# Graph attention, then masked attention: the first stage of x with VectorE transposes and seven block products for both matrices

## The chip, the cores and the metric

The kernel runs on one core of a Trainium2 chip, as one launch. The core has TensorE (matmuls, into PSUM), VectorE, ScalarE and GpSimd (elementwise work; in profiles DVE, ACT and POOL), and SyncE (SP), from which most DMAs of this kernel are issued. The metric is the device time of one execution in microseconds (us); lower is better. All data are 32-bit floats unless a smaller type is named.

## The reference

Two layers over 4096 nodes with 512 features, and an adjacency matrix of 4096 x 4096 zeros and ones. Cut to what is computed:

```python
# layer 0: graph attention, H = 4 heads of D = 128
support = (x @ weight).reshape(N, H, D).transpose(1, 0, 2)
f1 = einsum('hnd,hdo->hn', support, weight_u)[:, None, :]
f2 = einsum('hnd,hdo->hn', support, weight_v)[:, :, None]
logits = f1 + f2
w = where(logits >= 0, logits, 0.2 * logits)
masked = w * adj[None]; mask = masked != 0
attn = softmax(where(mask, masked, -1e30), axis=-1) * mask
out = einsum('hij,hjd->hid', attn, support) -> (N, H * D)
x1 = layernorm(x + out + bias + x @ proj_w + proj_b)
# layer 1: 8 heads of 64, keys, queries and values of x1, masked by adj with its diagonal
scores = einsum('hqk,hmk->hqm', x1 @ Wq, x1 @ Wk) / 8
att = softmax(scores + 0.01 * eye - 1e16 * (1 - max(adj, eye)))
result = layernorm(x1 + einsum('hqm,hmk,hko->qo', att, x1 @ Wv, Wo))
```

The change concerns the first two products, `x @ weight` (the support) and `x @ proj_w` (the projection), the two dot products of the support with `weight_u` and `weight_v`, and the sum x + bias + projection + proj_b (here the base).

## The kernel before, in words

The order of all instructions is written by hand: `tc.manual_schedule()` keeps, on each engine and on each DMA queue, the order in which the Python code issues them. An engine that waits for a semaphore holds everything behind it. A helper `later.at(n, fn)` puts work off by n steps, and `later.step()` counts the steps and issues what is due.

**First stage (lines 638 to 893).** x is worked in 8 groups of 512 rows (`for g in range(NG)`), each of 4 tiles of 128 rows. `load_x` brings 4 tiles with 4 DMAs, two groups ahead. `turn_x` (726) makes the transposed x of the next group: TensorE transposes 128x128 blocks into PSUM, VectorE and ScalarE copy them out in turn. For the first group the support is four plain products per tile (871). For the seven others it is seven block products instead of eight (Strassen's scheme, `block_product`, 807): x is cut in 2x2 blocks (row half, feature half), as is the weight, each product is 4 matmuls of 256 columns, and sums of blocks are formed before (`combine_x` on VectorE, 784; `combine_w` on GpSimd, 754) and after (ScalarE 823 and 827, GpSimd 825 to 834, VectorE 836). The projection (877) is 16 matmuls of 512 columns a group, and its base is made of the PSUM result and x plus bias, which GpSimd has added before (853), in one VectorE sum (886).

`dots` (795) multiplies a block of the support by the vectors (801, 512 wide) and reduces it (803), twice a block (weight_u, weight_v), all on VectorE.

`factors` (665) follows at the end of each group. ScalarE takes exponentials of the dot sums (669 to 680), VectorE notes their range (682, 683), GpSimd scales the support by them (685 to 689), SP stores it. Three steps later (`rest`, 694) the row factors are transposed by TensorE, copied and stored.

`beside` sets further work at given tiles: GpSimd starts DMAs that turn the adjacency into 16 bits (`narrow`, 585), SP transposes it by DMA (591), ScalarE turns it into 8 bits (597). At tile 30 the first three steps of the next stage are prepared (`front`, 617).

**Second stage (L1016 and its helpers)**: 4 windows of 1024 rows x 4 heads = 16 passes of 32 steps. In each step VectorE makes the weights p (633, 628) from ScalarE's signs (624), and TensorE multiplies them with the scaled support. `add_base` (980) adds the base by an accumulating DMA, `close` normalises. **Third stage**: keys, queries and values, then masked attention; the change does not touch it.

## Time and profile before

| what | before |
|---|---|
| median of 3 runs | 3380.09 us (3379.16 to 3389.31) |
| span of the profiled execution, first to last instruction | 3376.2 us |
| TensorE busy | 3351.0 us, 99% |
| VectorE busy | 2405.8 us, 71% |
| ScalarE busy | 1991.2 us, 59% |
| GpSimd busy | 2244.8 us, 66% |
| mean granted TensorE clock | 0.997 |
| first stage ends on TensorE | 232.2 us from the span's start |
| second stage runs without a gap from | 245.4 us |

The profile gives one execution's span; no time of its own is listed beside it for that execution. The median of the runs shown is 3.9 us above the span. Lines of the profile name an instruction by its line in the kernel, its engine, and the tiles it writes and reads (`out<-in`). In the timeline the columns are start, duration, engine, line, operation and, in brackets, how long the engine had been idle and what released it. A duration reaches from start to end, and the next instruction on the same engine may begin before that end. TensorE's work on 32-bit floats shows two records for each matmul.

### The profile page before, as it was taken

What the parts mean: (1) busy time and instruction counts of PE and PEld (TensorE: products, weight loads), DVE (VectorE), ACT (ScalarE), POOL (GpSimd) and SP (SyncE); (2) the same over time, 40 slices, a digit from 0 to 9 for tenths busy, and PEclk for the clock granted to TensorE, in tenths of its full rate; (3) what the DMA queues carried; (4) which work ended last, traced back from release to release, by engine and by line L of the source; (5) the groups of instructions that cost most, each with busy time, mean ns of one, the idle gap of its engine ahead of it and who ended that gap; (6) DMA issues with size and microseconds to landing.
All of it is one profiled execution on the core that took longest, in us unless ns stands there. A gap on an engine that the chain in (4) does not pass through costs nothing.

```text
span 3376.2 us, 66035 instructions
## 1 busy us (share of the span) xinstructions
PE 3351.0 (99%) x26970; PEld 1921.4 (57%) x26970; DVE 2405.8 (71%) x2485; ACT 1991.2 (59%) x2468; POOL 2244.8 (66%) x1592
## 2 busy tenths in 40 slices
PE   9999999999999999999999999999999999999998
PEld 5669999999999855543333333333333333333332
DVE  6889899998898721157766767666676666667676
ACT  1347877878876421156665656656566656656564
POOL 5650021030030174569999999999999999999996
PEclk9999999999999999999999999999999999999999
DMA  7989979769451263388989898899989889898884
GB/s 192 202 157 159 183 195 213 172 141 210 132 163 64 42 210 111 115 223 193 211 193 223 223 212 194 201 207 233 215 190 211 195 199 254 192 211 192 205 198 111
DMA packets 397129, 620.36 MB, mean 184 GB/s; under 512 B 165520, under 2 KB 242576, under 8 KB 395792
## 3 DMA queue, kind: packets, MB, share of 16 engines
q0 software_dynamic: 97376, 258.50, 42.2%
q1 hardware_dynamic: 298912, 356.49, 35.4%
q8 instruction: 214, 3.51, 0.4%
q10 hardware_dynamic: 528, 1.05, 0.1%
q14 instruction: 99, 0.81, 0.1%
HBM read 315.87 MB, written 117.64 MB: 128 GB/s over the span
## 4 chain that ended last, share of the span: by engine, by line
PE 97%; DVE 1%; DMA 1%; ACT 0%; POOL 0%; issue 0%; SPq 0%; POOLq 0%; DVEq 0%
PE o_ps L1016 27%; PE o_ps L1329 26%; PE s_ps L1067 26%; PE s_ps L1132 5%; PE s_ps L1393 3%; PE o_ps L877 3%; PE s_ps L1125 3%; PE o_ps L818 2%; DMA wq<-in_L_gnn_Wqs_dram 1%; PE s_ps L1348 1%; PE o_ps L871 0%; PE x_ps L997 0%; PE x_ps L735 0%; DVE p L1461 0%; PE x_ps L1125 0%; DVE x_sb L784 0%
## 5 line engine op out<-in xcount | busy, mean ns | idle before, releaser
L1304 POOL TENSOR_TENSOR q_sum<-q_sum,p 128x1024 f32<-128x1024 f32 x538 | 1375.8, 2557 | 62.2 <-DMA p<-p 39.0
L1284 DVE TENSOR_TENSOR p<-s_ps,adjT 128x1024 f32<-128x1024 f32 x896 | 1043.7, 1216 | 466.2 <-ACT s_ps L1281 443.4
L1281 ACT ACTIVATE s_ps<-s_ps 128x1024 f32<-128x1024 f32 x1021 | 967.1, 1006 | 594.5 <-PE s_ps L1067 594.3
L1329 PE MATMUL o_ps<-p,v_sb 64*64 64x512 f32 x8192 | 943.6, 590 | 0.0
L1067 PE MATMUL s_ps<-q_sb,k_sb 64*64 64x512 f32 x8192 | 942.7, 589 | 0.0
L1016 PE MATMUL o_ps<-sup_t,p 128*128 128x129 f32 x8192 | 922.3, 275 | 3.9 <-DVE p L633 3.9
L1016 PEld LDWEIGHTS o_ps<-sup_t,p 128*128 128x128 f32 x8192 | 919.7, 192 | 4.9 <-DVE p L633 3.9
L633 DVE SCALAR_TENSOR_TENSOR p<-fr_t,dj,az 128x1024 f32<-128x1024 f32 x512 | 654.6, 1288 | 80.9 <-PE o_ps L1016 53.5
L1329 PEld LDWEIGHTS o_ps<-p,v_sb 64*64 64x64 f32 x8192 | 310.3, 133 | 570.6 <-issue 560.3
L1067 PEld LDWEIGHTS s_ps<-q_sb,k_sb 64*64 64x64 f32 x8192 | 312.8, 133 | 565.9 <-issue 457.0
L624 ACT ACTIVATE z<-fr_t,f 128x1024 fp8e4<-128x1024 f32 x512 | 558.0, 1144 | 120.1 <-DVE az L628 119.7
L1314 POOL DMA_DIRECT2D p<-p x412 | 438.3, 1303 | 10.0 <-PE o_ps L1329 8.4
L980 POOL DMA_DIRECT2D agg<-base_d x32 | 28.6, 1201 | 526.8 <-ACT agg L967 526.6
L1284 DVE TENSOR_TENSOR p<-s_ps,md 128x1024 f32<-128x1024 f32 x128 | 150.5, 1217 | 67.3 <-ACT s_ps L1281 63.4
L628 DVE TENSOR_TENSOR az<-adjT,z 128x512 int32<-128x512 int32 x256 | 176.0, 688 | 4.1 <-ACT z L624 3.4
L584 POOL COPY seen<-token 128x1 f32<-128x1 f32 x24 | 14.0, 582 | 240.1 <-DVE token L582 240.1
L1139 ACT ACTIVATE sb<-s_ps 128x1024 f32<-128x1024 f32 x35 | 35.8, 1024 | 188.6 <-PE s_ps L1132 125.9
L597 ACT ACTIVATE adjT<-stage 128x1024 fp8e4<-128x1024 bf16 x128 | 130.9, 1050 | 4.5 <-DMA stage<-adj_d 4.5
L1154 POOL TENSOR_TENSOR sb<-sb,sb 128x1024 f32<-128x1024 f32 x36 | 84.4, 2359 | 71.7 <-ACT sb L1139 71.7
L877 PE MATMUL o_ps<-pw_sb,xT 128*128 128x512 f32 x256 | 115.1, 592 | 0.0
L1178 DVE COPY k_sb<-s_ps 128x1024 f32<-128x1024 f32 x12 | 14.7, 1224 | 139.2 <-PE s_ps L1132 89.5
L1393 PE MATMUL s_ps<-wo_sb,on 128*128 128x512 f32 x240 | 110.8, 604 | 0.0
(164 smaller groups left out, 2171.7 us busy)
## 6 DMA issues: line engine op xcount, KB each, us to landing
p<-p POOLq DMA_DIRECT2D x412, 512.0 KB, 9.1
k_sb<-k_d SPq DMA_DIRECT2D x128, 512.0 KB, 8.0
v_sb<-v_d SPq DMA_DIRECT2D x128, 512.0 KB, 5.9
adj_d<-in_adj_dram POOLq DMA_DIRECT2D x32, 1024.0 KB, 12.3
sup_t<-sup_d SPq DMA_DIRECT2D x120, 258.0 KB, 7.3
fr_t<-fr_d SPq DMA_DIRECT2D x16, 1024.0 KB, 7.5
adjT_d<-adjT SPq DMA_DIRECT2D x32, 512.0 KB, 4.5
adjT<-adjT_d SPq DMA_DIRECT2D x32, 512.0 KB, 6.7
```

The source lines that it names most:

```text
L624: nc.scalar.activation(z[:, k, :], fr[:, 0, :], AF.Sign, bias=fs[j // GT][:, 0, (j + k) % GT, h:h + 1], saturate=False)
L628: nc.vector.tensor_tensor(az.bitcast(I32), adjT[w, j // CJ][:, j % CJ:j % CJ + 2, :].bitcast(I32), z.bitcast(I32), op=ALU.bitwise_and)
L633: nc.vector.scalar_tensor_tensor(p, fr[:, 1, :], dj[j // GT][:, j % GT, h:h + 1], az_t[w, h, j // 2][:, j % 2, :], op0=ALU.max, op1=ALU.mult)
L877: nc.tensor.matmul(b_ps, xT[:, c, t * P:(t + 1) * P], pw_sb[c], start=(c == 0), stop=(c == KC - 1))
L1016: nc.tensor.matmul(o[t // BK][:, t % BK, :], p[:, t * P:(t + 1) * P], s, start=(j == 0 and t % BK == 0), stop=(j == NT - 1), skip_group_ch ...
L1067: nc.tensor.matmul(s[c:c + MS, e, :], k[r, a + c:a + c + MS], qt[g, m][r, :], start=True, stop=True)
L1281: nc.scalar.activation(s, s, AF.Exp)
L1284: nc.vector.tensor_tensor(p, s, keep[:, None, :].to_broadcast([P, HP, G]), op=ALU.mult)
L1304: nc.gpsimd.tensor_tensor(q, q, p, op=ALU.add)
L1314: later.at(2, lambda: nc.gpsimd.dma_start(a, b, accum_op=ALU.add))
L1329: nc.tensor.matmul(o[c, n, :], v[r, j % CH, c], p[r, e, :], start=(j == 0), stop=(j == NT - 1))
L1393: nc.tensor.matmul(s, on_t[g][:, m, t * P:(t + 1) * P], wo_sb[:, m, :], start=(m == 0), stop=(m == NP1 - 1))
```

## The change

1. x is loaded in another layout (`y_sb`): in blocks of 32 rows, four DMAs a group, so that four VectorE instructions, each transposing 32x32 blocks over 128x512, give the transposed x. The features lie in another order over the partitions, and the two matrices are loaded in the same order (eight DMAs each in place of four). TensorE transposes nothing in this stage.
2. Support and projection are both made by seven block products in all 8 groups, with a scheme that shares its sums (`product`): one set of four sums of x (two on VectorE, two on GpSimd) serves both matrices, and each matrix has four sums of weights. The order of the 14 products is in `usual`, and for the first group in `begin`.
3. The residual x is part of the projection: the identity is added to `proj_w` in 16 small GpSimd instructions at the start.
4. In `dots`, the multiplication by `weight_u` moves to GpSimd; the one by `weight_v` and both reductions stay on VectorE.
5. `factors` is put off by a step into the next group (after the fourth product), except in the last group. The row factors are transposed on VectorE in 32x32 blocks and stored with four DMAs.
6. bias and proj_b are no longer in the stage. In the first pass of the second stage, GpSimd issues eight accumulating DMAs that add their sum to the stored base, one per group.

```diff
-    base_d = [dram.tile([P, D], F32, name=f"base_d{i}") for i in range(NT)]
+    base_d = [dram.tile([P, GT, D], F32, name=f"base_d{g}") for g in range(NG)]
...
-            def load_x(g):
-                for t in range(GT):
-                    i = g * GT + t
-                    xs[i] = sp.tile([P, D], F32, name="x_sb", bufs=3 * GT)
-                    nc.sync.dma_start(xs[i], x[i * P:(i + 1) * P, :])
-            load_x(0)
-            for c in range(KC):
-                nc.sync.dma_start(w_sb[c], weight[c * P:(c + 1) * P, :])
-            for c in range(KC):
-                nc.sync.dma_start(pw_sb[c], proj_w[c * P:(c + 1) * P, :])
+            ys, xTs = {}, {}
+            def load_x(g, halves=1):
+                ys[g] = sp.tile([P, G // SQ, P], F32, name="y_sb", bufs=3)
+                nb = G // SQ // halves
+                for n in range(halves):
+                    r0 = g * G + n * nb * SQ
+                    for a in range(NQ):
+                        nc.sync.dma_start(
+                            ys[g][a * SQ:(a + 1) * SQ, n * nb:(n + 1) * nb, :],
+                            x[r0:r0 + nb * SQ, a * P:(a + 1) * P].rearrange(
+                                "(b r) f -> r b f", r=SQ))
+                    yield
...
+            halves = load_x(0, 2)
+            next(halves)
+            load_w0(w_sb, weight, 0)
+            next(halves)
+            load_w0(w_sb, weight, 1)
+            for c in range(2):
+                load_w0(pw_sb, proj_w, c)
             nc.sync.dma_start(uv[:, 0, :], on_all_partitions(weight_u, D))
             nc.sync.dma_start(uv[:, 1, :], on_all_partitions(weight_v, D))
-            nc.sync.dma_start(bb[:, 0, :], on_all_partitions(bias, D))
-            nc.sync.dma_start(bb[:, 1, :], on_all_partitions(proj_b, D))
-            load_x(1)
-            sums_of_w = wp.tile([P, 2, W], F32, name="fr_t").rearrange("p k r -> p (k r)")
-            last_fr = sums_of_w[:, 3 * D:4 * D]
+            list(load_x(1))
...
-                    nc.tensor.transpose(p, fr.rearrange("p k h t -> p (k h t)"), ident)
-                    if end:
-                        row = last_fr[0:n, P:2 * P]
-                    else:
-                        row = sp.tile([n, P], F32, name="fr_row")
-                    nc.vector.tensor_copy(row, p)
+                    n = 2 * H0 * GT
+                    row = sp.tile([P, n], F32, name="fr_row")
+                    nc.vector.transpose(row, fr.rearrange("p k h t -> p (k h t)"))
                     r0 = g * G % W
-                    nc.sync.dma_start(
-                        fr_d[g * G // W][:, :, r0:r0 + G].rearrange(
-                            "k h (t r) -> (k h) t r", r=P), row)
-                later.at(9 if end else 3, rest)
+                    dst = fr_d[g * G // W][:, :, r0:r0 + G].rearrange(
+                        "k h (t a r) -> a (k h) t r", a=NQ, r=SQ)
+                    for q in range(NQ):
+                        nc.sync.dma_start(dst[q], row[q * SQ:(q + 1) * SQ, :])
+                if g + 1 < NG:
+                    later.at(1, rest)
+                else:
+                    rest()
...
+            def turn_x(g, c, n=0, halves=1):
+                if c == 0 and n == 0:
                     xTs[g] = sp.tile([P, KC, G], F32, name="xT")
-                if g == 0:
-                    p = op.tile([P, G], F32, name="o_ps").rearrange("p (t r) -> p t r", t=GT)
+                nb = G // SQ // halves
+                nc.vector.transpose(
+                    xTs[g][:, c, n * nb * SQ:(n + 1) * nb * SQ].rearrange(
+                        "p (b r) -> p b r", r=SQ),
+                    ys[g][:, n * nb:(n + 1) * nb, c * SQ:(c + 1) * SQ])
...
-                for t in range(GT):
-                    nc.tensor.transpose(p[:, t, :], xs[g * GT + t][:, c * P:(c + 1) * P], ident)
-                dst = xTs[g][:, c, :]
-                if c % 2:
-                    nc.vector.tensor_copy(dst, p.rearrange("p t r -> p (t r)"))
-                else:
-                    nc.scalar.activation(dst, p.rearrange("p t r -> p (t r)"), AF.Copy)
...
+            def combine_w(engine, kind):
+                w = w_sb if kind == "s" else pw_sb
+                t1, t2, t3, t4 = sums_w[kind]
+                for dst, a, b in ((t1, w_block(w, 0, 1), w_block(w, 0, 0)),
+                                  (t2, w_block(w, 1, 1), t1),
+                                  (t3, w_block(w, 1, 1), w_block(w, 0, 1)),
+                                  (t4, w_block(w, 1, 0), t2)):
+                    engine.tensor_tensor(dst, a, b, op=ALU.subtract)
...
+                if i == 0:
+                    nc.vector.tensor_tensor(s[0], x_block(g, 1, 0), x_block(g, 1, 1), op=ALU.add)
+                elif i == 1:
+                    nc.vector.tensor_tensor(s[1], s[0], x_block(g, 0, 0), op=ALU.subtract)
+                elif i == 2:
+                    nc.gpsimd.tensor_tensor(s[2], x_block(g, 0, 0), x_block(g, 1, 0),
+                                            op=ALU.subtract)
+                    nc.gpsimd.tensor_tensor(s[3], x_block(g, 0, 1), s[1], op=ALU.subtract)
...
+            def dots(g, s4, n, m):
+                t, hs = slice(2 * n, 2 * n + 2), slice(2 * m, 2 * m + 2)
                 for k in range(2):
                     prod = sp.tile([P, D], F32, name="prod").rearrange(
-                        "p (t h d) -> p t h d", t=t.stop - t.start, d=D0)
+                        "p (t h d) -> p t h d", t=2, d=D0)
                     u = uv[:, k, :].rearrange("p (h d) -> p h d", h=H0)[:, None, hs, :]
-                    nc.vector.tensor_tensor(prod, s4[:, t, hs, 0:D0],
-                                            u.to_broadcast(list(prod.shape)), op=ALU.mult)
+                    engine = nc.vector if k else nc.gpsimd
+                    engine.tensor_tensor(prod, s4[:, t, hs, 0:D0],
+                                         u.to_broadcast(list(prod.shape)), op=ALU.mult)
                     nc.vector.tensor_reduce(fs[g][:, k, t, hs], prod, AX.X, ALU.add)
...
+                if i in (1, 5, 6):
+                    tiles[kind, i] = op.tile([P, G], F32, name="o_ps")
+                elif i == 7:
+                    tiles[kind, i] = xp.tile([P, GT, P], F32, name="x_ps").rearrange(
+                        "p t r -> p (t r)")
+                out = tiles[kind, {2: 1, 3: 5, 4: 7}.get(i, i)]
+                more = i in (2, 3, 4)
+                xb, wb = x_of(g, i), w_of(kind, i)
...
+                u2, p5 = sb[kind, 1], sb[kind, 5]
+                last = block_of(kind, s4, 1, 1)
+                if i in (1, 5):
+                    nc.scalar.activation(sb[kind, i], out, AF.Copy)
+                elif i == 2:
+                    nc.scalar.activation(block_of(kind, s4, 0, 0), as_block(out, kind), AF.Copy)
+                elif i == 6:
+                    nc.vector.tensor_tensor(u2, out, u2, op=ALU.add)
+                elif i == 7:
+                    nc.vector.tensor_tensor(last, as_block(out, kind), as_block(u2, kind),
                                             op=ALU.add)
+                    nc.gpsimd.tensor_tensor(last, last, as_block(p5, kind), op=ALU.add)
+                else:
+                    n, m = (0, 1) if i == 3 else (1, 0)
+                    nc.vector.tensor_tensor(block_of(kind, s4, n, m), as_block(out, kind),
+                                            as_block(u2, kind), op=ALU.add)
+                if i in (2, 3, 4, 7):
+                    n, m = {2: (0, 0), 3: (0, 1), 4: (1, 0), 7: (1, 1)}[i]
+                    if kind == "s":
+                        dots(g, s4, n, m)
+                    elif i in (3, 4):
+                        nc.sync.dma_start(base_d[g][:, 2 * n:2 * n + 2, :], base[n])
...
+            combine_w(nc.vector, "s")
+            for a in range(NQ):
+                q = slice(a * SQ, (a + 1) * SQ)
+                for c in range(KC):
+                    f = a * P + c * SQ
+                    d = pw_sb[q, c, f:f + SQ]
+                    nc.gpsimd.tensor_tensor(d, d, ident[q, q], op=ALU.add)
+            combine_w(nc.gpsimd, "b")
+            usual = [(k, i) for i in (1, 5, 2, 6, 7, 3, 4) for k in ("s", "b")]
+            begin = [("s", 1), ("s", 5), ("s", 2), ("s", 6), ("b", 1), ("s", 7), ("b", 5),
+                     ("s", 3), ("b", 2), ("s", 4), ("b", 6), ("b", 7), ("b", 3), ("b", 4)]
...
+                for k, (kind, i) in enumerate(usual if g else begin):
+                    if k in (0, 3, 6, 9):
+                        t = (0, 3, 6, 9).index(k)
+                        if t == 1 and g + 2 < NG:
+                            list(load_x(g + 2))
+                        for fn in beside.get(g * GT + t, []):
+                            fn()
+                        if g + 1 < NG:
+                            turn_x(g + 1, t)
+                    product(g, s4, kind, i)
+                    if g + 1 < NG and k >= 10:
+                        combine_x(g + 1, k - 10)
+                    if k in (3, 7, 10, 13):
+                        later.step()
                 xTs.pop(g)
+                x_s.pop(g)
+                if g + 1 < NG:
+                    later.at(1, lambda g=g, s4=s4: factors(g, s4))
+                else:
+                    factors(g, s4)
...
+        bb = turn_p.tile([P, KC, P], F32, name="x1T", bufs=4).rearrange("p c r -> p (c r)")
+        nc.sync.dma_start(bb, on_all_partitions(bias, D))
+        nc.gpsimd.dma_start(bb, on_all_partitions(proj_b, D), accum_op=ALU.add)
...
+                if n == 0 and j >= 6 and j % 3 == 0 and (j - 6) // 3 < NG:
+                    nc.gpsimd.dma_start(base_d[(j - 6) // 3],
+                                        bb[:, None, :].to_broadcast([P, GT, D]), accum_op=ALU.add)
```

## The prediction

> **What bounds the kernel now.** I read the page first, then the waits, the windows cut at the groups of the first stage, the timelines of each engine there, and last the chain at the stage's end.
>
> The page's first part (busy time of each engine) says that TensorE leaves nothing idle over the whole span of 3376.2 us:
> ```profile
> PE 3351.0 (99%) x26970; PEld 1921.4 (57%) x26970; DVE 2405.8 (71%) x2485; ACT 1991.2 (59%) x2468; POOL 2244.8 (66%) x1592
> ```
> The windows, cut at the start of each group of 512 rows, have the columns length, PE, weight loads, VectorE, ScalarE, GpSimd, clock, DMA share, GB/s:
> ```profile
> 67.80:95.50 27.70, 27.70 (x107) 18.38 (x106) 23.84 (x33) 4.86 (x11) 18.42 (x15) 1.00 0.88 193
> ...
> 178.50:206.20 27.70, 27.70 (x106) 18.38 (x105) 23.83 (x33) 8.41 (x15) 18.37 (x15) 1.00 0.83 163
> 206.20:232.20 26.00, 26.00 (x91) 16.77 (x90) 25.76 (x30) 11.48 (x17) 19.62 (x15) 1.00 0.64 117
> 232.20:245.40 13.20, 9.30 (x65) 8.84 (x64) 11.05 (x17) 6.89 (x11) 5.41 (x6) 0.82 0.94 194
> ```
> A group is 27.7 us of PE without a gap; VectorE is busy for 23.8 of them, so it is the next in line, with 3.9 to spare. The last row is the change of stages, where PE waits. The chain of waits gives what a piece of PE work is worth:
> ```profile
> 42.01 3.43 PE o_ps L877 x8
> 45.44 0.44 PE x_ps L735 x4
> 45.88 3.46 PE o_ps L818 x16
> ```
> Eight records (4 matmuls in two passes) of 512 columns are 3.43, four transposes 0.44, two block products 3.46, so 1.73 each. Before: 4 x 3.43 + 4 x 0.44 + 7 x 1.73 = 27.6, as the windows say.
>
> VectorE's timeline gives its rhythm, GpSimd's and ScalarE's the prices there:
> ```profile
> 93.52 0.68 DVE L836 TENSOR_TENSOR s<-o_ps,z 128x512 f32<-128x512 f32 x1
> 94.24 0.69 DVE L801 TENSOR_TENSOR prod<-s,uv 128x512 f32<-128x512 f32 x1
> 94.97 0.69 DVE L803 TENSOR_REDUCE f<-prod 128x4 f32<-128x512 f32 x1
> 95.57 0.68 DVE L801 TENSOR_TENSOR prod<-s,uv 128x512 f32<-128x512 f32 x1
> ...
> 98.27 6.98 DVE L784 TENSOR_TENSOR p<-xT 128x512 f32<-128x512 f32 x5
> ...
> 114.26 1.26 POOL L834 TENSOR_TENSOR z<-z 128x512 f32<-128x512 f32 x1
> ...
> 123.44 0.21 ACT L669 ACTIVATE aj<-f 128x16 f32<-128x16 f32 x1 [6.90 <-DVE f L803]
> 123.71 0.28 POOL L685 COPY sup_t<-aj 128x4 f32<-128x4 f32 x1 [8.19 <-DMA stage<-adj_d]
> 124.08 1.04 POOL L689 TENSOR_TENSOR sup_t<-s,aj 128x512 f32<-128x512 f32 x1
> 125.09 3.95 POOL L689 TENSOR_TENSOR s<-s,aj 128x512 f32<-128x512 f32 x3
> ```
> Start to start, a 512-wide VectorE instruction takes 0.60 (94.97 to 95.57), or 0.72 when the next one reads its result. The same work on GpSimd takes 1.26 with VectorE idle. In this kernel nothing on VectorE waits for GpSimd but the base sum (10.0 us in all in the waits), and the scaling of the support (L685, L689: 0.37 + 4.92, from 123.71 to 129.00) is waited for by no engine, only by stores.
>
> At the stage's end the chain runs:
> ```profile
> 238.10 0.70 DVE f L803
> ...
> 239.17 1.89 ACT adjT L597 x2
> 241.06 2.09 ACT z L624 x2
> 243.17 0.70 DVE az L628
> ...
> 245.40 10.13 PE o_ps L1016 x80
> ```
> PE restarts for good 6.6 us after the last dot sum of the stage (238.8); that work is the same afterwards. So the question is when the last dot sum ends.
>
> **TensorE.** Removed: 4 x 3.43 of projection and 4 x 0.44 of transposes in a group; added: 7 x 1.73. It has 14 x 1.73 = 24.2 a group, 3.4 less. Were PE still the bound, seven groups would save 24.
>
> **VectorE, counted.** A group has 4 transposes, 2 sums of x, 8 sums out of PSUM, 4 multiplications, 8 reductions and small ones: 26 large instructions at 0.60 to 0.72, about 17, below PE's 24.2. Counted by engine the change looks good. GpSimd has 4 dot products, 2 last sums, 2 sums of x and 4 scalings at 1.04 to 1.35, with the copies and a DMA issue 16 to 17, also below.
>
> **The ring of waits.** The order on the queues spoils it. The first multiplication of every dot goes to GpSimd, and VectorE's next instruction is the reduction of that product; VectorE stands until it is there. On GpSimd the scaling of the group before (now put one step later, behind the fourth product) lies ahead of the new group's first dot product. That scaling needs ScalarE's exponential, which needs the last GpSimd-fed reduction of the group before. So each group's first reduction waits for the last one of the group before and all between: a closed ring, which no slack in PE shortens. Around it once, from the end of the fourth dot product:
> - reduction, multiplication, reduction 1.92, last base sum 0.68; ScalarE's copy of the fifth projection product waits for that sum (it takes its buffer), 0.55, and the exponential is behind it, 0.28. GpSimd meanwhile does two sums of x (2.52) and the adjacency issue (0.80), so it is ready as ScalarE is: 3.5.
> - GpSimd: copies and scaling 0.37 + 4.92, first dot product 1.26: 6.55. VectorE has only two transposes and two small reductions under this.
> - VectorE: 1.92, one transpose 0.60, sums 6 and 6 1.20, small transpose 0.20, sum 7 0.72: 4.64. Then GpSimd: last sum 1.35, dot product 1.26: 2.61.
> - VectorE: 1.92, transpose 0.60, sum 0.68: 3.2. GpSimd: last sum, dot product 2.61 (VectorE's next sum is hidden).
> - VectorE: 1.92, sums of x 0.60 + 0.72, base 0.60, sum 0.68: 4.52. GpSimd: dot product 1.26.
>
> 3.5 + 6.55 + 4.64 + 2.61 + 3.2 + 2.61 + 4.52 + 1.26 = 28.9; eight changes of engine at some 0.05 (GpSimd's 115.52 to VectorE's 115.56) make 29.3, against 27.7. PE then waits about 5 us a group. After a wait of 3.7 us its next 16 records took 3.81 rather than 1.80; 24.2 + 2.0 is still below 29.3, so the clock doesn't decide.
>
> Bounds of the ring: with all GpSimd work at its cheapest row (1.04, L689) it is 2.3 shorter, with the transposes at 0.20 (the small row copy, 231.79 to 231.99) 0.8: 26.2. With GpSimd's dot products and last sums at 1.55 (mean of L833, beside VectorE's reads) 1.6 more, transposes and sums of x at 1.48 (mean of L784, beside GpSimd) 3.4 more, multiplications at 1.04 (L801, beside GpSimd) 1.3 more: 35.6. I take the prices without contention, since in the ring one of the two mostly stands while the other works.
>
> The block transpose has no row. The nearest is the reduction, also one 512-wide SBUF source, so 0.60. The Trainium skill ("VectorE: DVE Perf Modes", "The three transpose paths") gives 311 ns for 128x128 in a 16-bit type, which speaks against it: as an estimate 1.24 for 128x512, 0.64 more for each of two in the ring, with which the sum below would be about 10 us higher. No run here shows it yet.
>
> **The start.** SP issues 24 loads ahead of the dot vectors where it had 12. At the 0.46 of the rows (four in 1.85) the last of the projection's leaves at 11.8 and lands 5.6 later (median of these loads), at 17.4. GpSimd then adds the identity in 16 small instructions (0.20, as L686: 3.2), forms four weight sums (5.0) and only then the first dot product: 27.0. From there the same prices: VectorE 3.84, GpSimd 2.6, VectorE 3.2, 1.3, 3.2, 1.3 and 0.3 for the changes of engine end the group's fourth dot product at 42.7; base sums until 46.6, last sum, two sums of x and the issue until 51.3, scaling and first product of the second group 6.55: 57.9. Unsure by 4 either way (loads in 512-byte pieces).
>
> **The end.** Six rings: 57.9 + 6 x 29.3 = 233.7. Group 8 from there: VectorE 1.97, the five early instructions of the next stage 5.1, sums 2.1, GpSimd 2.7, VectorE 2.6, 2.7, 3.2, 1.4, and the last dot 2.0: 23.8. Last dot sum 257.5 against 238.8: **+18.7**.
>
> **What else moves.** Bias: two loads fewer early; two later, and eight accumulating issues of 1 MB on GpSimd in the first pass of stage two, where GpSimd is busy 5.35 of 57.6: at 1.2 to 2.6 each hidden. Their traffic: the software queue took 42.2% of the span for 258.5 MB, 5.5 us a MB, so 46 us for 8.4 MB, where a DMA share of 0.78 leaves 13. Loads of the next pass land in 6.8 to 8.8 and are issued some 30 us ahead, so I take 0; worst case 11. The row store becomes four DMAs (0.67 each on SP, 2.0 more a group), base stores half as many; x has 4 x as many pieces, loaded a group ahead. Behind these on SP stands the adjacency transpose, needed more than a group later. Hidden: 0.
>
> Sum against the profiled span: 3376.2 + 18.7 = 3394.9. The median shown is 3.9 above that span: 3380.1 + 18.7, **3399 us**.
>
> **Rivals.**
> 1. PE stays the bound (the ring runs under 24.2), and the kernel is faster. For it: both engines are below 24.2 by count. Against: 5 us would have to go from prices read with the other engine idle. Then the first projection product starts at 20.6 (17.4 + 3.2), ten products of 1.73 end the first group at 37.9, and 7 x 24.2 and the same change of stages (13.2, the last window) follow: 220.5 against 245.4, so 3355. Chance 0.08.
> 2. The ring near its low bound, 26.2 to 27.8: 6 x 1.5 to 3.1 less, so 0 to +10: no difference to speak of, 3380 to 3390. Chance 0.16.
> 3. The ring with contention, 32 to 34: +35 to +47, 3415 to 3427. Two-input reads on both engines at once speak for it, their taking turns against. Chance 0.18.
> 4. The accumulating DMAs delay the loads of the second pass: +11 on top. Chance 0.05.
>
> The forecast's own case, 29.3 within 1.3, has 0.53. A difference of 0.3% (10 us) is what a measurement of this kernel can tell. Faster by more: 0.08 (rival 1). Within: 0.16. Slower: 0.76. The range leaves out rival 1 and the tail above ring 33: 3378 to 3424.
>
> **What would show it.** The reduction (line 820 of the changed kernel) waiting for GpSimd's product at 818, longest at each group's first; the exponentials 29 us apart, now 27.7; PE idle about 5 us a group, its clock no longer 1.00; stage two starting near 264. Wrong if the exponentials are 24 apart, or if the reductions wait for PE.

## The result, and the profile after

| what | before | after |
|---|---|---|
| median | 3382.02 us (3379.16 to 3389.31, 4 runs) | 3407.28 us (3406.51 to 3408.11, 4 runs) |
| span of the profiled execution | 3376.2 us | 3404.6 us |
| first stage: last dot sum ends | 238.8 us | 254.7 us |
| second stage on TensorE without a gap from | 245.40 us | 261.26 us |
| second stage's last matmul starts | 1164.6 us | 1189.7 us |
| third stage's first score matmul starts | 1455.4 us | 1480.5 us |

The changed kernel is slower: the ratio is 1.0073, interval 1.006 to 1.0085. The table says where the 28.4 us between the two spans arise: 15.9 by the end of the first stage, 9.2 more in the second (928.4 us from its start to its last matmul, 919.2 before), nothing at the change to the third (290.8 in both), and 3.3 after that (most likely a trait of the one execution profiled before; see the part on why).

The 15.9 are not spread over the groups. From the end of the second group's last dot sum to that of the seventh's it is 138.4 us before (69.30 to 207.72) and 140.3 after (84.46 to 224.79). The first group's last dot sum ends 2.7 us later (44.33 against 41.64), the step from there to the second group's takes 40.1 instead of 27.7, and the last group is 1.1 shorter. So in between the groups have kept their length, though TensorE has 3.4 us less to do in each, and the loss against the kernel before lies in the step from the first group to the second.

First the changed kernel's page, its first part (busy time of each engine) and the group of the reductions (the last columns are idle time just before them and what ended it):

```profile
PE 3339.6 (98%) x27050; PEld 1958.6 (58%) x27050; DVE 2361.8 (69%) x2476; ACT 1985.7 (58%) x2461; POOL 2233.7 (66%) x1614
...
L820 DVE TENSOR_REDUCE f<-prod 128x4 f32<-128x512 f32 x64 | 43.9, 686 | 90.8 <-POOL prod L818 89.7
```

TensorE, VectorE, ScalarE and GpSimd all have less to do than before, and the kernel is slower. VectorE stands 89.7 us before reductions whose product GpSimd has not delivered. The timelines of the changed kernel give one group (start, duration, engine, line, operation, idle time and releaser): ScalarE's exponential, GpSimd behind it, VectorE behind GpSimd.

```profile
113.47 0.21 ACT L685 ACTIVATE aj<-f 128x16 f32<-128x16 f32 x1
141.34 0.21 ACT L685 ACTIVATE aj<-f 128x16 f32<-128x16 f32 x1
...
141.61 0.19 POOL L696 COPY sup_t<-aj 128x4 f32<-128x4 f32 x1 [0.31 <-ACT aj L685]
...
119.34 0.69 DVE L820 TENSOR_REDUCE f<-prod 128x4 f32<-128x512 f32 x1 [5.08 <-POOL prod L818]
...
126.20 0.69 DVE L820 TENSOR_REDUCE f<-prod 128x4 f32<-128x512 f32 x1 [2.37 <-POOL prod L818]
...
131.83 0.69 DVE L820 TENSOR_REDUCE f<-prod 128x4 f32<-128x512 f32 x1 [1.83 <-POOL prod L818]
...
137.68 0.69 DVE L820 TENSOR_REDUCE f<-prod 128x4 f32<-128x512 f32 x1 [1.45 <-POOL prod L818]
```

The exponentials are 27.86, 27.83, 27.87, 28.93, 27.86, 27.74 and 27.59 us apart (57.78 to 253.46), and each group's longest wait is that at its first reduction. GpSimd picks up the exponential 0.3 us after it had become idle: each link is there when the next one needs it. The windows between exponentials (length, PE, weight loads, VectorE, ScalarE, GpSimd, clock, DMA share, GB/s):

```profile
85.64:113.47 27.83, 24.43 (x106) 20.89 (x105) 16.98 (x31) 7.57 (x15) 14.96 (x15) 0.94 1.00 190
113.47:141.34 27.87, 26.15 (x122) 22.70 (x121) 17.00 (x31) 7.75 (x16) 14.98 (x15) 1.00 1.02 190
141.34:170.27 28.93, 25.52 (x106) 21.65 (x105) 17.77 (x33) 7.47 (x15) 14.98 (x15) 0.88 1.12 207
```

PE is 1.7 to 3.4 us idle in these three groups, and its clock falls below 1.00 in two of them. No engine is full, as counted; VectorE has 17.0 and GpSimd 15.0 of the 27.9, and each stands while the other makes what it needs. The last columns hold something that the prediction did not use for this stage: the share of the 16 DMA engines is 1.00 and more.

In the second stage, the timelines of PE, ScalarE and SP of the changed kernel:

```profile
261.26 126.98 PE L1054 MATMUL o_ps<-sup_t,p 128*128 128x129 f32 x1120 [1.86 <-DVE p L637]
394.75 132.59 PE L1054 MATMUL o_ps<-sup_t,p 128*128 128x129 f32 x1168 [6.51 <-DVE p L637]
...
389.45 1.06 ACT L601 ACTIVATE adjT<-stage 128x1024 fp8e4<-128x1024 bf16 x1 [10.89 <-DMA stage<-adj_d]
...
319.40 71.56 SPq L595 DMA_TRANSPOSE stage<-adj_d  x3
```

Its DMA issues, with KB each and the median time from issue to landing:

```profile
adj_d<-in_adj_dram POOLq DMA_DIRECT2D x32, 1024.0 KB, 14.6
base_d<-x1T POOLq DMA_DIRECT2D x8, 1024.0 KB, 33.4
```

In the profile before, the same transposes and the longest such wait in that place were these:

```profile
390.96 1.06 ACT L597 ACTIVATE adjT<-stage 128x1024 fp8e4<-128x1024 bf16 x1 [3.34 <-DMA stage<-adj_d]
...
301.15 70.64 SPq L591 DMA_TRANSPOSE stage<-adj_d  x3
```

In the changed kernel ScalarE waits 10.89 us for a transposed block of the next window's adjacency; its signs for the current window stand behind that, VectorE's weights behind the signs, and PE stands still for 6.51 us. In the ten us after (395 to 405) it gets through 74 matmul records at a clock of 0.81, against 92 in a full stretch: 2 us more. The eight bias DMAs took 33.4 us to land (median).

### The profile page after: what moved, and what is told of

It reads as the page before. It is cut to its first block, busy times and chain, and to the rows that moved or that the text cites. A ratio compares the mean times of both kernels' runs of the same rounds, so it can differ in the third digit from the quotient of the medians.

```text
span 3404.6 us, 66196 instructions
## 1 busy us (share of the span) xinstructions
PE 3339.6 (98%) x27050; PEld 1958.6 (58%) x27050; DVE 2361.8 (69%) x2476; ACT 1985.7 (58%) x2461; POOL 2233.7 (66%) x1614
## 3 DMA queue, kind: packets, MB, share of 16 engines
q1 hardware_dynamic: 309904, 356.23, 34.9%
## 4 chain that ended last, share of the span: by engine, by line
PE 73%; issue 7%; POOL 6%; DMA 5%; DVE 1%; SPq 1%; ACT 0%; POOLq 0%; DVEq 0%
PE o_ps L1367 22%; PE s_ps L1105 21%; PE o_ps L1054 18%; PE s_ps L1170 5%; POOL q_sum L1342 3%; PE s_ps L1431 3%; PE s_ps L1163 3%; DMA p<-p 3%; DMA stage<-adj_d 1%; SPq L595 1%; POOL p L1352 1%; PE s_ps L1386 0%; POOL q_sum L1338 0%; DMA sup_t<-sup_d 0%; DMA xT<-x1T_d 0%
## 5 line engine op out<-in xcount | busy, mean ns | idle before, releaser
L601 ACT ACTIVATE adjT<-stage 128x1024 fp8e4<-128x1024 bf16 x128 | 130.9, 1051 | 15.9 <-DMA stage<-adj_d 15.9
L820 DVE TENSOR_REDUCE f<-prod 128x4 f32<-128x512 f32 x64 | 43.9, 686 | 90.8 <-POOL prod L818 89.7
```

## The experiments

Each kernel is the changed one with the edits shown. "Groups" are the distances between the exponentials of the first stage. The kernel before, run again beside each set, had medians of 3382.2 to 3383.4 us, so gains of a microsecond or two between sets mean nothing.

**All dot multiplications on VectorE.**

```diff
-                    engine = nc.vector if k else nc.gpsimd
+                    engine = nc.vector
```

> The changed kernel with one edit: both multiplications of each dot product stay on VectorE. Theory (a closed ring VectorE, ScalarE, GpSimd sets the 27.9 us of a group): the ring is cut, VectorE has some 21 us a group by count (4 transposes of 0.62, 2 sums of x and 16 dot instructions of 0.66, 8 sums out of PSUM of 0.72, 0.7 of small ones), PE's 24.2 is the bound, the exponentials come 24.2 to 25.5 apart, and the first stage ends 18 to 26 us earlier; whole time 3381 to 3390. Rival (VectorE and GpSimd slow each other down, or VectorE is the true bound): with 2.7 us more on VectorE the groups stay at 27 to 30 us and the time at 3405 to 3420. The 9 us lost in the second stage stay in both.

Measured: 3390.22 us (ratio to before 1.0023, 1.001 to 1.0037), 17.1 less than the changed kernel; last exponential 239.4 instead of 253.5, so 14 us earlier, less than the 18 to 26 expected. Groups 25.2, 24.2, 24.2, 25.1, 31.4, 25.9, 28.0. The windows of this kernel:

```profile
104.75:128.93 24.18, 24.18 (x114) 21.29 (x113) 21.50 (x35) 7.70 (x15) 11.30 (x11) 1.00 1.25 193
128.93:154.06 25.13, 25.13 (x117) 21.85 (x116) 21.50 (x35) 7.82 (x16) 11.29 (x11) 1.00 1.17 225
154.06:185.49 31.43, 25.25 (x109) 21.27 (x108) 21.50 (x36) 7.68 (x15) 10.38 (x11) 0.95 1.25 182
```

Cutting the ring gives groups that PE fills (24.18 of 24.18), with 4.5 us more on VectorE. The theory of the ring stands, and the rival, which kept the groups at 27 to 30, is out. But one group takes 31.4 and two more take 25.9 and 28.0. ScalarE and SP in the group of 31.4:

```profile
161.67 0.60 ACT L868 ACTIVATE s<-o_ps 128x512 f32<-128x512 f32 x1 [7.07 <-DMA sup_d<-s]
170.80 0.60 ACT L868 ACTIVATE base<-o_ps 128x512 f32<-128x512 f32 x1 [8.53 <-DMA base_d<-base]
...
132.85 9.46 SPq L656 DMA_DIRECT2D y_sb<-in_x_dram  x4
...
146.26 2.76 SPq L703 DMA_DIRECT2D sup_d<-s  x3
...
152.76 14.78 SPq L595 DMA_TRANSPOSE stage<-adj_d  x1
```

The copy into the support's buffer waits for the store of the group before last, with the DMA engines at 1.25. That store stood on SP behind the four loads of x, which held SP for 9.46 us, left it by 149.0 and had not landed for 12 us more. The base copy then waits for a store that did stand behind the transpose of 14.78. A second limit lies right under the first.

**The scaling behind the first dot product instead of ahead of it.**

```diff
-                    later.at(1, lambda g=g, s4=s4: factors(g, s4))
+                    later.at(2, lambda g=g, s4=s4: factors(g, s4))
```

> The changed kernel with one edit: the exponentials and GpSimd's scaling of the group before come four products later, behind the new group's first dot product and ahead of its second. GpSimd multiplies as much as in the changed kernel. Theory (what closes the ring is the scaling ahead of the first dot product, waiting for the last sum of the group before): the ring opens, since the scaling then waits for nothing late; VectorE trails PE by some 5 us but is not tied to its own last group; groups at 24.3 to 25.5 us, the first stage 16 to 24 us shorter, whole time 3383 to 3391. Rival (the dot products on GpSimd cost the time by themselves, wherever the scaling stands): VectorE still waits some 10 us a group, groups at 27 to 28, time within 3 us of 3407.

Measured: 3409.23 us, no gain. The time is the rival's, but the groups are not: 24.2, 34.9, 26.0, 34.4, 24.8, 28.3, and 20.0 for the last. The first three windows:

```profile
62.02:86.26 24.24, 24.24 (x114) 21.35 (x113) 16.91 (x29) 3.78 (x11) 14.57 (x15) 1.00 0.83 135
86.26:121.19 34.93, 34.65 (x161) 30.16 (x161) 22.05 (x38) 7.72 (x15) 16.40 (x16) 1.00 1.17 198
121.19:147.19 26.00, 17.12 (x66) 14.28 (x65) 12.76 (x21) 7.70 (x16) 14.98 (x15) 0.80 0.97 159
```

PE fills the first. In the second it still works while the exponential is late, and it pays in the third (17.12 of 26.00). Another late exponential, on ScalarE, GpSimd and SP:

```profile
181.08 0.60 ACT L868 ACTIVATE base<-o_ps 128x512 f32<-128x512 f32 x1 [10.38 <-DMA base_d<-base]
...
181.85 0.19 POOL L696 COPY sup_t<-aj 128x4 f32<-128x4 f32 x1 [9.79 <-ACT aj L685]
...
159.63 11.24 SPq L595 DMA_TRANSPOSE stage<-adj_d  x1
```

A base copy waits for the store of the group before, which left SP only after the adjacency transpose; the exponential stands behind that copy on ScalarE, and VectorE waits over 11 us for GpSimd. So the expectation was wrong on the time and, as far as one group shows it, right on the ring: the first of these groups, which no store held, took 24.24 us with as many multiplications on GpSimd as in the changed kernel, whose first takes 27.86. (With the scaling moved in the same way further below, the first group takes 24.23.) What the ring gave back, transfers took.

**Without the eight accumulating DMAs of the bias.**

```diff
-                if n == 0 and j >= 6 and j % 3 == 0 and (j - 6) // 3 < NG:
-                    nc.gpsimd.dma_start(base_d[(j - 6) // 3],
-                                        bb[:, None, :].to_broadcast([P, GT, D]), accum_op=ALU.add)
```

> The changed kernel without its eight accumulating DMAs of the bias (bias and proj_b are thus left out of the base; their two loads stay). The first stage is as in the changed kernel (groups of 27.9 us, last dot sum near 254). Theory (the accumulations hold the software queue, GpSimd's adjacency DMAs behind them land late, ScalarE waits for the transposed adjacency and PE idles 6.5 us near 395 with a lower clock after): the wait of 10.9 us on ScalarE is below 4, and the time falls by 7 to 11 us, to 3396 to 3400. Rival (the second stage's loss comes from something else that moved, such as the four-piece row stores or the later start against the same traffic): it falls by less than 3 us.

Measured: 3400.7 us, 6.6 less, without the bias in the result. PE in the second stage:

```profile
260.72 256.17 PE L1051 MATMUL o_ps<-sup_t,p 128*128 128x129 f32 x2288 [1.86 <-DVE p L637]
```

It has no gap for 256.17 us, the second stage takes 918.6 us, as before the change (919.2), and ScalarE's waits for transposed blocks in it are 0.3 us in all instead of 15.9. The adjacency DMAs issued at 280, 292, 304 and 318 land after 10.0, 8.4, 11.5 and 23.6 us here; in the changed kernel those issued in the same stretches land after 30.4, 43.8, 50.6 and 43.3. That is the mechanism, and the whole of the second stage's 9.2. (The next one lands after 33.5 without the bias and 39.5 with it, and in the kernel before the first three of this window took 8.5 to 12.4 and the other five 19.8 to 33.3: late landings there are not new, and what is new is that the first are late too.) The gain shows less in the whole time because this execution spends 5.3 us more behind the second stage (1929.4 us from the third stage's first score matmul to the end, against 1924.1).

**The same eight DMAs later, one every six steps in the third and fourth pass.**

```diff
-                if n == 0 and j >= 6 and j % 3 == 0 and (j - 6) // 3 < NG:
-                    nc.gpsimd.dma_start(base_d[(j - 6) // 3],
+                if w == 0 and u >= 72 and u % 6 == 0 and (u - 72) // 6 < NG:
+                    nc.gpsimd.dma_start(base_d[(u - 72) // 6],
```

> The changed kernel with the eight accumulating DMAs moved from the first pass of the second stage to its third and fourth, one every six steps, behind the last of the adjacency DMAs of that window. Same traffic, another place. Theory (their place in the queue ahead of the adjacency costs the time): PE's wait near 395 is gone and the time falls by 7 to 11 us, as without them, to 3396 to 3400. Rival (the traffic costs it, wherever it lies): the wait is gone but comes back in the third or fourth pass, with loads or stores late, and the time falls by less than 4 us.

Measured: 3437.16 us, 30 more than the changed kernel. Neither text foresaw that. PE and SP:

```profile
429.44 17.02 PE L1054 MATMUL o_ps<-sup_t,p 128*128 128x129 f32 x128 [27.29 <-DVE p L637]
459.81 104.74 PE L1054 MATMUL o_ps<-sup_t,p 128*128 128x129 f32 x912 [13.34 <-DVE p L637]
...
317.45 90.41 SPq L595 DMA_TRANSPOSE stage<-adj_d  x3
```

For the first five GpSimd had nothing to wait for: right after the window's last adjacency DMA, at 367.5, it sent five of the eight in 6.2 us, whatever steps stood between them in the code. The eight landed after 52.2 us (median). The two adjacency DMAs issued just ahead of them, at 354 and 367, landed after 32.1 and 31.1 us (20.9 and 14.1 without the bias), SP's transposes were late, and ScalarE waited 33.11 us for one. So standing ahead in the queue did not keep these two from landing late, and it hit the place with the least slack harder. How much of the two delays is the burst's is not shown: the adjacency DMA issued at 329, well ahead of it, landed after 25.7 us here and after 33.5 without the bias.

**Bias by GpSimd at the end of each window.** Each finished tile gets bias plus proj_b by an addition of 128x512 on GpSimd, and there are no accumulating DMAs into the stored base.

```diff
+                y = agg_t[w][:, t].rearrange("p h d -> p (h d)")
+                nc.gpsimd.tensor_tensor(y, y, bb[0], op=ALU.add)
-                nc.gpsimd.dma_start(agg_t[w][:, t].rearrange("p h d -> p (h d)"),
-                                    base_d[i // GT][:, i % GT, :], accum_op=ALU.add)
+                nc.gpsimd.dma_start(y, base_d[i // GT][:, i % GT, :], accum_op=ALU.add)
```

> The changed kernel with the bias in another place: no accumulating DMAs into the stored base; in each window of the second stage GpSimd adds bias plus proj_b (two small loads a window) to each finished tile, 32 additions of 128x512 near 1.3 us, where GpSimd has little else. First stage untouched: groups of 27.9 us. Theory (the 1 MB accumulations ahead of the adjacency DMAs in the software queue made them land after 30 to 51 us instead of 8 to 24): adjacency lands as without bias, no wait of PE near 390, time 3398 to 3403, as without the bias at all (3400.7). Rival (the additions at a window's end delay the layer norm and what follows): 3404 to 3412.

Measured: 3436.94 us, 30 more, though the wait near 390 is gone. (Two of the four runs took 3430 and 3431 us, two 3443; the profile is of one of these.) The loss is at the ends of the windows. VectorE there, and GpSimd:

```profile
487.38 4.62 DVE L637 SCALAR_TENSOR_TENSOR p<-fr_t,dj,az 128x1024 f32<-128x1024 f32 x2
491.92 2.02 DVE L632 TENSOR_TENSOR az<-adjT,z 128x512 int32<-128x512 int32 x1
494.05 5.38 DVE L637 SCALAR_TENSOR_TENSOR p<-fr_t,dj,az 128x1024 f32<-128x1024 f32 x2
...
489.34 1.56 POOL L1022 TENSOR_TENSOR agg<-agg,x1T 128x512 f32<-128x512 f32 x1
```

The same lines without additions on GpSimd beside them (the kernel without bias):

```profile
485.74 2.48 DVE L637 SCALAR_TENSOR_TENSOR p<-fr_t,dj,az 128x1024 f32<-128x1024 f32 x2
488.14 0.69 DVE L632 TENSOR_TENSOR az<-adjT,z 128x512 int32<-128x512 int32 x1
```

Two weights take 4.62 to 5.38 instead of 2.48, the mask 2.02 instead of 0.69. From the first to the last transposed tile of the stage it is 790.7 us against 757.1: 11.2 for each of three windows. The Trainium skill ("SBUF — State Buffer", "SBUF: two separate sides") says that a VectorE instruction with two SBUF inputs and a GpSimd instruction that reads SBUF exclude each other for the whole of an instruction; these rows agree, the mask's 1.33 of delay being most of one addition's 1.56.

**Three edits together: dot products on VectorE, that bias, and the adjacency transposes three quarters of a group later on SP; the same with a third base buffer; and the scaling moved, with the same two.**

```diff
-                beside.setdefault(4 * c + 7, []).append(lambda c=c: turn_in0(0, c))
+                beside.setdefault(min(4 * c + 10, NT - 1), []).append(lambda c=c: turn_in0(0, c))
```

> Three edits: all dot multiplications on VectorE, the bias on GpSimd at the end of each window, and in the first stage the adjacency's DMA transpose issued three quarters of a group later on SP, behind the stores of support and base of that group. With the dot products on VectorE alone, four groups ran at 24.2 to 25.2 us, and then ScalarE waited 7.07 and DVE 7.46 us for a store of the support that stood on SP behind a transpose of 14.8 us. Theory (the second limit is SP's order, stores behind a transpose that waits for its adjacency block): the exponentials come 24.2 to 25 apart in all groups, the stage ends some 10 to 14 us earlier than with the dot products on VectorE alone, time 3366 to 3374, below the kernel before. Rival (the traffic of a group doesn't fit 24.2 us, the DMA share being 1.0 to 1.1 at 27.8): the waits come back elsewhere, loads of x or transposes late, groups at 26 to 28, time 3378 to 3386.

> As the kernel before in this list (dot products on VectorE, bias on GpSimd, transpose later), with three buffers for the base instead of two. If stores of the base still hold ScalarE's or VectorE's copies after the transposes are out of the way, this gains 2 us or more on it; if SP's order was the whole of it, the two are within 2 us.

> Multiplications by weight_u stay on GpSimd as in the changed kernel; the scaling comes four products later (behind the first dot product), the bias is added by GpSimd in the second stage, and the adjacency transposes stand three quarters of a group later on SP. With the scaling moved alone, groups took 24.2, 34.9, 26.0, 34.4, 24.8, 28.3 us: in the long ones ScalarE waited about 10 us for a store of the base behind a transpose. Theory (ring opened, SP's order the next limit): groups 24.3 to 26 us in all, time 3370 to 3380. Rival (GpSimd's and VectorE's alternation costs 27 us by itself): groups 27 to 28, time 3396 to 3402.

Measured: 3441.95, 3438.42 and 3435.18 us; all three carry the loss of the GpSimd additions, so only their groups say something. They were 25.2, 32.9, 24.4, 42.5, 25.1, 23.8, 23.6 in the first of them, 25.2, 29.9, 25.4, 37.8, 24.5, 24.6, 23.3 with the third buffer, and 24.2, 29.0, 25.6, 34.3, 23.1, 28.8, 19.8 with the scaling moved. The wait is now at the other end of the transpose (ScalarE in the first of the three):

```profile
175.30 2.00 ACT L601 ACTIVATE adjT<-stage 128x1024 fp8e4<-128x1024 bf16 x2 [34.26 <-DMA stage<-adj_d]
```

The order on SP is thus not the second limit: with the stores let ahead, the adjacency is late instead. The expected 3366 to 3374 were far off for two reasons, the additions and this. (The first of the three texts puts the wait of 7.07 us for a support store down to the transpose of 14.8; in the lines of the first experiment that store left SP ahead of the transpose.) The third buffer's 3.5 us are too few to say that stores of the base held anything, since the runs of the two kernels overlap (3438 to 3446 and 3436 to 3442).

**The bias DMAs spread, two in each window** (steps 6 and 12 of the first window, 13 and 15 of the others, ahead of that window's adjacency; the sum of the two biases is loaded once a window); alone, with the dot products on VectorE, and with more buffers as well.

```diff
+                for k in range(2):
+                    if u == ((13, 15) if w else (6, 12))[k]:
+                        nc.gpsimd.dma_start(base_d[2 * w + k],
+                                            bb[0][:, None, :].to_broadcast([P, GT, D]),
+                                            accum_op=ALU.add)
...
-                s4 = sp.tile([P, GT, H0, W0], F32, name="s4")
+                s4 = sp.tile([P, GT, H0, W0], F32, name="s4", bufs=3)
...
-                            base[n] = sp.tile([P, 2, D], F32, name="base", bufs=2)
+                            base[n] = sp.tile([P, 2, D], F32, name="base", bufs=3)
```

> The changed kernel with the eight accumulating DMAs of the bias spread: two in each of the four windows, for the two groups of rows that the window needs, ahead of the window's adjacency DMAs (steps 6 and 12 of the first window, 13 and 15 of the others), and the small bias loads once a window. Same traffic in all, nothing left out. Theory (eight of them together held the software queue and with it the adjacency): adjacency DMAs land as without bias, PE has no wait above 2 us in the second stage, time 3398 to 3403 (3400.7 without the bias). Rival (any accumulation in the queue costs its own time once): 3405 to 3410.

> The spread bias and all dot multiplications on VectorE. The two gains measured alone are 17 (dot products on VectorE) and 6.7 us (no bias accumulations). If they add: 3382 to 3386, level with the kernel before. If the waits for the DMA engines (their share was 1.04 to 1.25 in the groups of 24 to 25 us) decide the first stage, its groups again take 24.2 us in some and up to 31 in others, 26.3 in the mean.

> As the one before in this list, with three buffers for the scaled support and for the base instead of two, and two for x instead of three, so that no copy waits for a store of the group before. Theory A (the long groups come from too few buffers for stores that land late): all groups 24.2 to 25.5 us, 8 to 12 us less, 3372 to 3378. Theory B (the DMA engines can't carry a group's 4.9 MB in 24.2 us, whatever the buffers): the wait moves, to the adjacency or to x, mean group 25.8 or more, gain under 4 us.

Measured: spread alone 3399.91 us (ratio 1.0049, 1.003 to 1.0067); PE runs from 261.03 for 257.41 us without a gap, a bias DMA lands after 11.8 us instead of 33.4 (median of the eight), and the four adjacency DMAs after 21.4, 14.9, 11.7 and 21.6 instead of 30.4 to 50.6. With the dot products on VectorE 3384.48 us (1.0005, 0.9995 to 1.0015): the two gains add, 22.8 of 17.1 + 7.4. With more buffers 3382.97 us (1.0003, 0.9989 to 1.0018), 1.5 less, which is within the spread of the runs. No version up to here is faster than the kernel before; these two are level with it. ScalarE with more buffers:

```profile
168.12 2.00 ACT L601 ACTIVATE adjT<-stage 128x1024 fp8e4<-128x1024 bf16 x2 [12.39 <-DMA stage<-adj_d]
196.77 2.00 ACT L601 ACTIVATE adjT<-stage 128x1024 fp8e4<-128x1024 bf16 x2 [12.01 <-DMA stage<-adj_d]
```

The waits for stores of the base on ScalarE (8.56 and 10.95 us with fewer buffers) have become waits for the adjacency of 12.39 and 12.01, in the same two groups. The mean group is 25.4 and 25.3 (theory B expected 25.8 or more, so they are a little better than that, but the gain and the moved wait are B's).

**The same without the larger buffers, x in rows of 2 KB.**

```diff
-                    for a in range(NQ):
-                        nc.sync.dma_start(
-                            ys[g][a * SQ:(a + 1) * SQ, n * nb:(n + 1) * nb, :],
-                            x[r0:r0 + nb * SQ, a * P:(a + 1) * P].rearrange(
-                                "(b r) f -> r b f", r=SQ))
+                    for a in range(NQ // halves):
+                        t = n * NQ // halves + a
+                        r0 = g * G + t * P
+                        nc.sync.dma_start(
+                            ys[g][:, t * NQ:(t + 1) * NQ, :].rearrange("p b f -> p (b f)"),
+                            x[r0:r0 + P, :])
```

> Dot multiplications on VectorE and the spread bias, but x is loaded in whole rows of 2 KB, four DMAs a group as in the kernel before, in place of pieces of 512 bytes. The block transposes then give another order than the products need, so the values aren't those of the reference; bytes, instructions and waits are as in the same kernel with 512-byte pieces. If the pieces are what fills the DMA engines (the hardware queue took 4.9 us of 16 engines a MB in the changed kernel's first stage, 4.4 before), the DMA share falls by 0.1 or more, the long groups go and the time is 6 to 12 us lower than with the pieces. If the bytes decide, it is within 3 us.

Measured: 3372.36 us (ratio to before 0.9971, 0.9957 to 0.9985), 12.1 less than with pieces of 512 bytes. Its values are in another order, so it measures a time and is no version to use. Its windows, and below them the same two stretches with the pieces:

```profile
127.30:151.48 24.18, 24.18 (x114) 21.29 (x113) 21.57 (x35) 7.70 (x16) 11.29 (x11) 1.00 1.12 227
151.48:175.65 24.17, 24.17 (x114) 21.28 (x113) 21.48 (x35) 7.70 (x15) 11.27 (x11) 1.00 1.23 219
175.65:199.41 23.76, 23.76 (x112) 20.92 (x111) 21.07 (x35) 7.59 (x15) 11.28 (x11) 1.00 1.18 216
```

```profile
152.95:181.93 28.98, 25.66 (x112) 22.02 (x111) 21.45 (x35) 7.69 (x15) 10.38 (x11) 0.94 1.21 186
181.93:209.33 27.40, 24.44 (x114) 21.20 (x113) 20.01 (x32) 7.70 (x15) 10.84 (x11) 1.00 1.14 204
```

From the second on, no group takes more than PE's 24.2 (the first takes 25.2), with the same bytes and instructions. The DMA share in the groups is about as high as with the pieces (expected was a fall by 0.1), but those engines move 216 to 219 GB/s instead of 186 to 204. Between 55 and 235 us the hardware queue took 78.8% of the 16 engines' time for 28.97 MB, against 85.1% for 27.94 MB with the pieces: 2.72 and 3.05 points a MB. That is not the price of pieces alone, for the changed kernel, with pieces and with longer groups, is at 2.74 (70.6% for 25.76 MB). So x in small pieces is what stretched the groups, by 12.1 us in all. By which way is not shown: the pieces took more of the DMA engines' time, and they also held SP, where the stores stand behind the loads of x. In the group from 129 us on, the four loads held SP for 10.07 us with pieces and 2.66 with rows. No run takes the two apart. The Trainium skill ("DMA: Bandwidth & Descriptors", "Specifications") gives 512 bytes as the smallest transfer that keeps the line rate; in these runs, pieces of just that size cost more than pieces of 2 KB.

## Why the prediction was right, and where it was not

The sum said 3394.9 us of span and 3399 in the median; it came to 3404.6 and 3407.3. The direction and the mechanism of the first stage were right; that the bias would cost nothing was wrong. Term by term:

- **The ring of waits: right.** Cutting it by where the product is made, and opening it by where the scaling stands, both gave groups of 24.2 us where no transfer held them (two, three and four in a row with the one, in the first, the spread and the row experiments; only the first group with the other). The signs came in part: the reductions waited, longest at each group's first, and the clock fell, but the exponentials are 27.9 apart and not 29, and PE idles 1.0 to 4.3 us a group and not 5.
- **Its length: 29.3 predicted, 27.9 measured.** Six rings took 28.0 in the mean. The mis-sized term is GpSimd's work with VectorE idle. Three scalings took 3.05 us, not the 3.95 read from a stretch where VectorE was busy; the last sums 1.09 and 1.27, not 1.35. From the second group's first reduction (63.65) to the eighth's (231.75) it is 168.1 us instead of 175.8, so **-7.7**.
- **The block transpose: right.** It is 0.70 us long and 0.62 from start to start (121.27 to 121.89), against 0.60 taken. The estimate of 1.24 from the 311 ns of the Trainium skill ("VectorE: DVE Perf Modes", "The three transpose paths") was too long here; the row decides.
- **The start: 57.9 predicted, 63.6 measured, +5.7.** The identity additions took 0.31 each rather than 0.20, but the weights landed earlier, and the first group's last dot product starts its reduction at 42.32, as said (42.7). The step that failed came next: the sum took ScalarE's exponential as waiting for the base sums and GpSimd alone. PE, ScalarE, VectorE and GpSimd at that place:

```profile
46.27 3.75 PE L849 MATMUL x_ps<-more_w,xT 128*128 128x256 f32 x8 [8.20 <-DVE base L872]
...
57.78 0.21 ACT L685 ACTIVATE aj<-f 128x16 f32<-128x16 f32 x1
...
63.65 0.69 DVE L820 TENSOR_REDUCE f<-prod 128x4 f32<-128x512 f32 x1 [11.53 <-POOL prod L818]
...
58.06 0.19 POOL L696 COPY sup_t<-aj 128x4 f32<-128x4 f32 x1 [7.01 <-ACT aj L685]
```

PE waited 8.20 us for a PSUM buffer that VectorE's base sum held behind two dot products; the next group's products came late, ScalarE's four copies of them with it, and the exponential stands behind those copies. GpSimd, ready at 51.0, waited 7.01 for it. This step is where the stage loses against the kernel before, and the ring is only a small part of it: from the first group's last dot sum to the second's it takes 37.4 us in the first experiment and 37.8 with rows, where the ring is cut, against 40.1 in the changed kernel.

- **The last group: 23.8 predicted, 23.0 measured, -0.8.** Together -2.8: the stage ends 15.9 later than before, 18.7 was said, and PE restarts at 261.26, not "near 264".
- **"What else moves ... I take 0": wrong, +9.2.** The bias DMAs were priced by their bytes and by the loads of the next pass. No wait of PE in the stage was for loads. The adjacency DMAs of the next window are issued among and behind them on the same queue; the profile before shows these (12.3 us to landing in the page's median, up to 33.3 in this window) and SP's three transposes of 70.64 us, and ScalarE already waiting 3.34 us for a transposed block. That was the thin place, and it was not looked at. Rival 4, the accumulating DMAs at +11, had the size and 0.05 of the chance, but another victim. The other term put at 0, x in four times as many pieces, cost nothing here, where the ring sets the group; with the ring cut and the bias spread the pieces cost 12.1 us.
- **3.3 us after the second stage: most likely the execution that was profiled before.** The code there is the same. From the second stage's last transposed tile to the end it is 2117.2 us in the one profile of before, 2120.5 after, and 2119.5 to 2125.8 in the twelve experiments. In all runs listed with a span, the time is 1.7 to 2.2 us above it. So the profiled execution before, with its 3376.2, would be one of some 3378 us, below each of the four runs shown and 4 below their median, while that of the changed kernel is 0.8 below its own. The medians differ by 25.3, which is the 15.9 and the 9.2. Why an execution ends sooner there was not settled; that PE waits there for VectorE's weights more in some is seen (2.4 us after, 6.2 without the bias).
- **The rivals.** PE as the bound (3355) was refuted for the change as made; it comes into reach only when the dot products, the bias and the pieces of x are all undone, and then gives 3372, not 3355: the first group ends some 10 us later than that sum assumed (PE restarts at 230.81, and 7 x 24.2 and 13.2 before that is 48.2, not 37.9), and the later stages hold the rest. The ring with contention happened in one place of a ring only (at 138 a multiplication of 1.14 us instead of 0.68, beside a sum of x on GpSimd of 1.72 instead of 1.26), since elsewhere one engine stands while the other works; it happened at once where GpSimd was given work beside a busy VectorE (4.62 to 5.38 for 2.48). The ring near its low bound (26.2 to 27.8) missed by 0.1 us a group; the measured ring is at the lower edge of the forecast's own case (29.3 within 1.3).

So the difference of the medians, 25.3 instead of 18.7, is off by 6.6, the sum of misses of both signs: -2.8 in the first stage and +9.2 in the second. (The forecast of 3399 also stood on a median before of 3380.1 from three runs; with the fourth it is 3382.0.) That the total came this near is luck: the six rings were taken 7.7 too long, the start 5.7 too short, and the cost of the bias was missing.

## What to carry to other kernels

An engine's count of busy time says nothing about a period: follow one result from engine to engine, and if the path comes back to where it started one group later, the period can't be shorter than its length, whatever slack each engine has. Follow the first result through once more by itself: here the step from the first group to the second cost more than the ring. Before an engine is relieved, read the DMA share of that stage: at 0.83 to 1.00 for 27.7 us, this one left little room for 24.2, and smaller pieces took what there was. Work put on a queue is priced by what stands next to it and by the consumer with the least slack there, not by its own bytes.

## What the runs showed of the hardware that was not expected

- Accumulating DMAs of 1 MB land after 33.4 us when eight are issued in 21 us, after 52.2 when five are issued in 6.2, and after 11.8 in pairs (medians of the eight). The four adjacency DMAs issued among and right behind the eight needed 30 to 51 us instead of 8 to 24.
- GpSimd's additions with two SBUF inputs, 1.56 us each, about doubled VectorE's time beside them (4.62 to 5.38 for 2.48) and cost 11.2 us for the eight of a window.
- A VectorE block transpose of 128x512 32-bit values takes 0.70 us, 0.62 from start to start, as much as a reduction of that width.
- x in pieces of 512 bytes instead of 2 KB cost the kernel 12 us, with the same bytes.
